# A fused decoder layer: the state sums on two column tiles of TensorE, the heads spread by pairs of chunks and sequence, and the second head's turning placed behind the first quadrants

## The chip, the core and the metric

The kernel runs on one core of a Trainium2 chip. The time is the device time of one execution in microseconds (us). The engines are TensorE (PE in the profile, its weight loads PEld), VectorE (DVE), ScalarE (ACT), GpSimd (POOL) and SyncE (SP), which issues most DMAs. The kernel before took 1444.93 us, the median of three runs (1443.88 to 1446.36).

## The reference, cut to what matters

A post-norm decoder layer over 16 sequences of 256 tokens with 512 features, in float32. Each of three sublayers is added to its input and layer-normalised.

```python
# 1: a state-space mixer inside
xn = x * rsqrt(mean(x*x)) * w_norm
z, xi, dt, B, C = split(xn @ W_in.T)           # z, xi: 1024 wide; dt: 16 heads; B, C: 16 heads x 16 states
xi = silu(causal_conv4(xi)); dt = softplus(dt + dt_bias); dA = exp(dt * -exp(A_log))
u = (dt * mean_over_64_channels(xi))[..., None] * B
h_t = dA_t * h_(t-1) + u_t                     # a scan along the tokens of a sequence
y_t = sum over the 16 states of h_t * C_t      # 16 heads per token
y = (y @ W_h2i.T) * silu(z)                    # 16 heads -> 1024 channels
out = y @ W_out.T + x
# 2: a long convolution along the 512 features, per position in a head of 8 tokens
# 3: x @ W.T + b + a top-2 mixture of 8 rank-16 updates
```

What the change touches most are the three lines of the sum over the states, the spreading of 16 heads to 1024 channels, and the gate by `silu(z)`.

## The kernel before, in words

**First stage** (span 0 to about 771 us). The 4096 tokens go in eight groups of 512, that is two sequences of 256 at a time. For each group ten pairs of products (`first_products`, `last_products`, line 309) make `xi`, `z`, `B` and `C`, with the channels (or the heads' states) on the 128 partitions and the 512 tokens along the free axis. They are Strassen-like products of 256 columns each. A product of two chunks of `z` is called a pair `p`; its chunks are `2p` and `2p+1`. The order of the ten pairs is a list in the code (lines 576, 577), and each step issues, by hand, the first products of its own pair, the last products of the pair before, and the vector work between. No scheduler reorders anything: each engine takes its instructions in the order in which the code issues them.

Three small steps sit between these products on TensorE:

- `head_means` (line 550) makes means over 64 channels, with weights of 32 columns, in four column tiles of the array side by side.
- The state sums, `yps` (line 611). After the scan, `Bs[ht]` holds the products of state and `C` for 8 heads x 16 states on 128 partitions (`ht` is 0 or 1). A 0/1 matrix `sel` adds up the 16 states of each head. It has four copies of the 32 columns, so the 128 output partitions hold the same sums four times. These are two matmuls of the full array, 512 columns each. ScalarE copies the result to `yT` (line 639).
- `spread_heads(cc)` (line 668), once for each half of the 1024 channels. Chunk `4cc+q` takes rows `32q` to `32q+31` of `yT` (copy `q`) against 32 rows of `w_h`, in four row tiles side by side, into four PSUM banks. `gated` (line 681) multiplies each chunk of `z` with one bank on VectorE.

Then comes the output projection (line 709), again in the Strassen-like form, and the layer norm. The eighth group has nothing to overlap with, so it uses the plain product (line 795) over four token tiles in the order 0, 2, 1, 3, then VectorE adds the residual and normalises (`L810`, `L61`, `L501`), and SP stores to DRAM. Within the fourth tile TensorE also turns (transposes) the first head's input, `turned_v`, line 146; ScalarE copies it (line 148), and VectorE makes its products with the context (line 158).

**Second stage** (from about 771 us). Over 32 heads: a convolution as a Toeplitz product, `convolve`, for each of two halves of the batch. It has twelve *quadrants* (64 x 64 tiles, line 977) and full-array matmuls (line 959). In the first half of the first head (`late`) the quadrants come first and six full matmuls (`FIRST`) behind them. VectorE then contracts the result with the context (lines 1010 and 1020). A head's input is loaded by `load_v` (one buffer, so the next load waits for the turning of the last), turned, and multiplied one head ahead. Before the first head's loop begins, the second head's input is turned (line 1108), and then the third head's input and context are loaded.

PSUM has eight banks: two of `ps_t` (tag `tr`), and in the first stage two of `ps_s` and four of `ps_mm` (`bank()`). In the second stage the two of `ps_b` and the four of `ps_y` (the tiles `y0` and `y1`) take the place of the last six.

The lines that the change and the steps of the prediction touch:

Of the kernel before, what the change touches and what calls it, by code (L numbers as in the profile page):

```python
# [14 lines left out]
P = 128  # L15
# [4 lines left out]
NI = DI // P  # L20
# [51 lines left out]
def decoder_kernel(  # L72
# [63 lines left out]
    def load_v(h):  # L136
        vn = q3.tile([P, D], F32, tag="vn", name="vn", bufs=1)
        sh, hs = divmod(h, P // NH)
        nc.sync.dma_start(vn, first[sh][:, hs * NH : (hs + 1) * NH, :])
        return vn  # L140
# [30 lines left out]
    with ExitStack() as s1:  # L171
# [3 lines left out]
        p2 = s1.enter_context(tc.tile_pool(name="p2", bufs=2))  # L175
        gp = s1.enter_context(tc.tile_pool(name="gp", bufs=NI))
        ps_s = s1.enter_context(tc.tile_pool(name="ps_s", bufs=2, space=PSUM))
# [70 lines left out]

        w_h = w1.tile([P, 2, P], F32, name="w_h")
        nc.gpsimd.memset(w_h, 0.0)  # L250
        for q in range(4):
            nc.sync.dma_start(
                w_h[32 * q : 32 * q + H1],
                Wh2iT.rearrange("h (cc q i) -> q h cc i", q=4, i=P)[q],
            )
# [44 lines left out]

        sel = w1.tile([P, HT, 4, 2 * H1], F32, name="sel")
        nc.gpsimd.memset(sel, 0.0)

        def bank():
            return ps_mm.tile([P, 512], F32, tag="mm", name="mm")
# [142 lines left out]
        for ht in range(HT):  # L448
            for q in range(4):
                nc.vector.tensor_reduce(  # L450
                    sel[:, ht, q, ht * HH : (ht + 1) * HH],
                    ident.rearrange("p (h n) -> p h n", n=NST),
                    AX.X,
                    ALU.add,
                )
# [51 lines left out]
        for g in range(NG):  # L507
# [5 lines left out]

            accs, zs, silus = [], [], []

            def places(kind, p):

                if kind == "x":
                    two = [t[:, :, 3:] for t in (xis[2 * p % 4], xis[2 * p % 4 + 1])]
                    return [t[:, b, :] for t in two for b in range(GB)]  # L520
                if kind == "z":
                    two = [gp.tile([P, GT], F32, tag="zs", name="zs") for _ in range(2)]
                    zs.extend(two)
                else:
                    two = [p2.tile([P, GT], F32, tag=kind, name=kind) for _ in range(2)]
                    (Bs if kind == "b" else Cs).extend(two)
                return [t[:, b * S : (b + 1) * S] for t in two for b in range(GB)]
# [69 lines left out]
            for i, (kind, p) in enumerate(order):  # L597
# [9 lines left out]
                if i == 9:  # L607

                    yps = ps_t.tile([P, GT], F32, tag="tr", name="yps")
                    for ht in range(HT):  # L610
                        nc.tensor.matmul(  # L611
                            yps,
                            sel[:, ht].rearrange("p q h -> p (q h)"),
                            Bs[ht],
                            start=(ht == 0),
                            stop=(ht == HT - 1),
                        )
                if before is not None:
# [18 lines left out]
                if i == 9:  # L637
                    yT = q3.tile([P, GT], F32, tag="vn", name="yT", bufs=1)
                    nc.scalar.copy(yT, yps)
# [24 lines left out]
            def spread_heads(cc):  # L664
                pss = []
                for q in range(4):
                    ps = bank() if q < 2 else ps_t.tile([P, GT], F32, tag="tr", name="wh")
                    nc.tensor.matmul(  # L668
                        ps,
                        w_h[32 * q : 32 * (q + 1), cc, :],  # L670
                        yT[32 * q : 32 * (q + 1), :],
                        start=True,
                        stop=True,
                    )
                    pss.append(ps)
                return pss

            def gated(cc, pss):
                for q in range(4):
                    z = zs[4 * cc + q]  # L680
                    nc.vector.tensor_tensor(z, z, pss[q], ALU.mult)

# [104 lines left out]
            else:  # L787
                finish_sums()
                gated(1, spread_heads(1))
                for n, t in enumerate((0, 2, 1, 3)):  # L790

                    ps = ps_s.tile([P, 512], F32, tag="s", name="s") if n == 0 else bank()
                    for c in range(NI):
# [43 lines left out]
    with ExitStack() as s2:  # L837
# [111 lines left out]

        def convolve(y, kv, T, Td, kvd, q, between=None, late=False, early=None):  # L950

# [48 lines left out]
            if late:  # L1000
                for n, (lb, mb) in enumerate(FIRST):
                    if n == 1 and early is not None:
                        early()
                    if n == 3 and between is not None:
                        between()
                    full(lb, mb, T[:, FULL_AT[lb, mb], :])
# [100 lines left out]
        more_next[3]()  # L1107
        vT_after = turned_v(vns.pop(0))
        vns.append(load_v(2))
        cTs.append(load_c(2))  # L1110

# [26 lines left out]
        for h in range(HX):  # L1138
# [33 lines left out]
            red = p2.tile([P, NQ, NL, BQ * NH], F32, tag="red", name="red")  # L1172
            convolve(y, kv, T, Td, kvd, 0, late=h == 0)
            ws = skip_sum(sk_next)
# [201 lines left out]
```

## Time and profile before

| | us |
|---|---|
| median of three runs | 1444.93 |
| the profiled execution's own time | 1447.89 |
| its span (first to last instruction) | 1446.1 |
| one group of the first stage, in the steady part | 92.45 |
| TensorE busy | 1425.9 (99%) |
| VectorE busy | 1215.7 (84%) |
| ScalarE busy | 464.4 (32%) |
| GpSimd busy | 567.8 (39%) |

The profiled execution is 1.8 us longer than its span, and 2.96 us above the median of the runs. Each float32 matmul of the program appears as two matmuls, two passes, in the profile: `yps` has 16 in the program and 32 in the profile. The mean duration of one matmul in a group includes the way out of the array and overlaps the next, so that what a matmul costs is read from the chain of waits, where pieces lie end to end: `PE mm L309 x16` in 3.45 us is 0.2156 us for a pass of 256 columns. The granted clock of TensorE is 0.998 of full speed.

### The profile page before, as it was taken

Reading aid. Unit: us, or ns where it says so; the run is one execution under the profiler, and the core shown is the slowest. Engines: PE = TensorE matmul, PEld = TensorE weight load, DVE = VectorE, ACT = ScalarE, POOL = GpSimd, SP = SyncE. Lnnn points to the kernel's source line nnn. Section 1 sums busy time; section 2 is a strip of 40 time slices with the busy share of each in tenths; the row PEclk is TensorE's granted clock in tenths of the full one; section 3 lists DMA queues with packets and bytes.
Section 4 is the critical chain, followed back from the end, with each engine's and each line's share of the span. In section 5 each row is a group of like instructions: output and inputs, shape, how many; then the busy total and the mean of one; then the engine's idle time right before and its main releaser. Section 6 shows DMA issues by size and latency. Waiting matters only on the chain.

```text
span 1446.1 us, 18895 instructions
## 1 busy us (share of the span) xinstructions
PE 1425.9 (99%) x6828; PEld 915.6 (63%) x6828; DVE 1215.7 (84%) x2093; ACT 464.4 (32%) x969; POOL 567.8 (39%) x662
## 2 busy tenths in 40 slices
PE   8999999999999999999999999999999999999997
PEld 8778788788887888878875444444444444444443
DVE  6877778878787787877857999999999999999996
ACT  2522223223233232332311333333333333333332
POOL 7340010020100201002004666776677666766772
PEclk9999999999999999999999999999999999999999
DMA  8014012111121111202103122212221222122210
GB/s 295 32 37 130 8 39 81 44 54 36 37 83 38 53 44 37 83 11 84 51 8 120 42 80 73 69 61 79 74 76 54 79 73 70 58 81 73 68 40 23
DMA packets 50815, 93.30 MB, mean 65 GB/s; under 512 B 10657, under 2 KB 15009, under 8 KB 50721
## 3 DMA queue, kind: packets, MB, share of 16 engines
q1 hardware_dynamic: 50192, 92.08, 19.9%
q8 instruction: 54, 0.88, 0.3%
q14 instruction: 41, 0.33, 0.1%
q10 hardware_dynamic: 528, 0.00, 0.0%
HBM read 74.75 MB, written 17.32 MB: 64 GB/s over the span
## 4 chain that ended last, share of the span: by engine, by line
PE 90%; DVE 6%; issue 1%; DMA 1%; ACT 1%; POOL 0%; SPq 0%; POOLq 0%; DVEq 0%; ACTq 0%
PE mm L309 18%; PE y L959 15%; PE s L309 12%; PE y L977 12%; PE base L1133 8%; PE s L709 6%; PE mm L709 5%; PE yc L947 4%; PE gl L1198 2%; PE base L1129 2%; DVE acc L540 2%; PE tr L1047 1%; PE mm L795 1%; PE mm L668 1%; PE yps L611 1%
## 5 line engine op out<-in xcount | busy, mean ns | idle before, releaser
L1010 DVE TENSOR_TENSOR pr<-y,cT 128x1024 f32<-128x1024 f32 x126 | 148.3, 1219 | 41.5 <-PE y L977 37.1
L977 PE MATMUL y<-kv 64*64 64x512 f32 x1408 | 180.8, 598 | 0.5 <-DVE xt L810 0.4
L158 DVE TENSOR_TENSOR kv<-vT,cT 128x1024 f32<-128x1024 f32 x128 | 180.0, 1447 | 1.4 <-ACT vT L148 1.4
L540 DVE SCALAR_TENSOR_TENSOR acc<-xi,wc,acc 128x512 f32<-128x512 f32 x192 | 145.9, 774 | 5.7
L1020 DVE TENSOR_REDUCE red<-pr 128x128 f32<-128x1024 f32 x126 | 147.1, 1208 | 0.0
L959 PE MATMUL y<-kv 128*128 128x512 f32 x272 | 128.1, 594 | 2.1 <-DVE pr L1010 1.2
L977 PEld LDWEIGHTS y<-kv 64*64 64x64 f32 x1408 | 51.5, 132 | 120.6 <-issue 91.0
L885 POOL TENSOR_TENSOR o<-t,vT 64x384 f32<-64x384 f32 x64 | 121.1, 1892 | 4.4
L1133 PE MATMUL base<-w_f,ol 128*128 128x512 f32 x248 | 119.5, 605 | 0.0
L959 PE MATMUL y<-kv,Td 128*128 128x512 f32 x248 | 116.5, 592 | 0.0
L357 POOL TENSOR_TENSOR rstd<-ms,nhalf 128x4 f32<-128x4 f32 x8 | 8.1, 1018 | 260.1 <-DVE ms L355 260.1
L67 POOL TENSOR_TENSOR rs_a<-ve_a,nhalf 128x1 f32<-128x1 f32 x32 | 19.0, 593 | 189.0 <-DVE ve_a L65 189.0
L309 PE MATMUL mm<-XT,w_z 128*128 128x256 f32 x384 | 90.7, 379 | 0.0
L959 PEld LDWEIGHTS y<-kv,Td 128*128 128x128 f32 x248 | 47.1, 190 | 59.3 <-issue 59.1
L959 PEld LDWEIGHTS y<-kv 128*128 128x128 f32 x272 | 49.0, 190 | 53.9 <-issue 50.6
L924 POOL TENSOR_TENSOR xs<-kv 128x512 f32<-128x512 f32 x63 | 80.4, 1276 | 2.4
L309 PEld LDWEIGHTS mm<-XT,w_z 128*128 128x128 f32 x384 | 73.0, 190 | 9.9
L1133 PEld LDWEIGHTS base<-w_f,ol 128*128 128x128 f32 x248 | 42.3, 189 | 54.5 <-issue 54.5
L948 ACT COPY y<-yc 128x1024 f32<-128x1024 f32 x62 | 61.8, 997 | 34.0 <-PE yc L947 23.8
L1165 POOL TENSOR_TENSOR ol<-o,red 128x512 f32<-128x512 f32 x31 | 39.5, 1273 | 83.3 <-DVE red L1020 83.3
L309 PE MATMUL mm<-xnT,w_z 128*128 128x256 f32 x288 | 70.4, 381 | 0.0
L977 PE MATMUL y<-kvd,kv 64*64 64x512 f32 x128 | 65.2, 589 | 0.0
(276 smaller groups left out, 2957.2 us busy)
## 6 DMA issues: line engine op xcount, KB each, us to landing
cT<-in_ctxT SPq DMA_DIRECT2D x32, 448.0 KB
kv<-in_toep SPq DMA_DIRECT2D x32, 448.0 KB
xt<-in_x SPq DMA_DIRECT2D x32, 256.0 KB
xnT<-in_xT SPq DMA_DIRECT2D x8, 1024.0 KB
spread<-both SPq DMA_DIRECT2D x32, 256.0 KB
first<-xt SPq DMA_DIRECT2D x32, 256.0 KB
vn<-first SPq DMA_DIRECT2D x32, 256.0 KB
out<-res SPq DMA_DIRECT2D x31, 256.0 KB
```

Source lines behind the costliest of these rows:

```text
L158: last = nc.vector.tensor_tensor(kv[:, q, k * BQ : (k + NL // 2) * BQ], vT[:, q, blks].rearrange("p k (b i) -> p (k b) i", i=NH).unsqueeze ...
L309: nc.tensor.matmul(ps, w[:, p, a, kc, :], Xs[b][:, kc, :], start=start and kc == 0, stop=stop and kc == 1, skip_group_check=upon,)
L540: nc.vector.scalar_tensor_tensor(acc, xi[:, :, k : k + S], wc[:, c, k : k + 1], acc, ALU.mult, ALU.add)
L709: nc.tensor.matmul(ps, own[a][c][:, n * P : (n + 1) * P], w_o[b][c], start=start and c == 0, stop=stop and c == HC - 1, skip_group_check=upon,
L885: nc.gpsimd.tensor_tensor(o[b : b + HP, :, 0:3], t[a : a + HP, :, 1:4], vT[a : a + HP, :, 1:4], ALU.add,)
L924: return nc.gpsimd.tensor_tensor(xs[:, q], moving(kv, q, 0), moving(kv, q, 1), ALU.add)
L948: nc.scalar.copy(y[1], yc.unsqueeze(1).to_broadcast([P, 2, BQ * NH * NH]))
L959: nc.tensor.matmul(bank_of(y, lb), w, moving(kv, q, mb), start=not late and lb not in begun, stop=False, skip_group_check=True,)
L977: return nc.tensor.matmul(bank_of(y, lb)[cols], T[rows, at, cols], src[rows], start=start, stop=False, skip_group_check=True,)
L1010: nc.vector.tensor_tensor(pr.rearrange("p (k b j) i -> p k b j i", k=2, j=NH), y[i].rearrange("p k (b j i) -> p k b j i", j=NH, i=NH), cT[ ...
L1020: nc.vector.tensor_reduce(red[:, q, 2 * i : 2 * i + 2, :].rearrange("p k t -> p (k t)"), pr, AX.X, ALU.add)
L1133: nc.tensor.matmul(base, o_l[:, kc, :], w_f[:, kc, :], start=(first and kc == kcs[0]), stop=False)
```

## The change

- **State sums.** `sel` keeps two copies of the 32 columns instead of four, so that a sum takes 64 columns of the array. Each of the two matmuls of 512 columns becomes two of 256: sequence 0 goes to column tile 0 (output partitions 0 to 63), sequence 1 to column tile 1 (64 to 127). `yps` and `yT` are 256 wide instead of 512.
- **Spreading.** A row tile `q` now stands for a sequence (`q // 2`) and a pair of chunks (`q % 2`). `w_h` holds two chunks for each row tile (loaded twice, once per sequence), and each row tile makes two matmuls of 256 columns in place of one of 512, into the two halves of its bank.
- **Gating.** The two chunks of a pair of `z` lie in one tile `[P, 2, 512]`, and `gated` multiplies, for one sequence, both chunks of a pair at once: 2 x 256 elements in place of 512 in a row.
- **The last group's fourth token tile** uses the free bank of `ps_s` in place of one of `ps_mm`.
- **The second head's turning**, with the two loads behind it, is issued behind the twelve quadrants of the first head's first half (a callback `ahead`), ahead of the six full matmuls, instead of before the quadrants.

```diff
-        gp = s1.enter_context(tc.tile_pool(name="gp", bufs=NI))
+        gp = s1.enter_context(tc.tile_pool(name="gp", bufs=NI // 2))
...
-        w_h = w1.tile([P, 2, P], F32, name="w_h")
+        w_h = w1.tile([P, 2, 2, P], F32, name="w_h")
         nc.gpsimd.memset(w_h, 0.0)
         for q in range(4):
             nc.sync.dma_start(
                 w_h[32 * q : 32 * q + H1],
-                Wh2iT.rearrange("h (cc q i) -> q h cc i", q=4, i=P)[q],
+                Wh2iT.rearrange("h (cc q e i) -> q h cc e i", q=2, e=2, i=P)[q % 2],
             )
...
-        sel = w1.tile([P, HT, 4, 2 * H1], F32, name="sel")
+        sel = w1.tile([P, HT, 2, 2 * H1], F32, name="sel")
...
-            for q in range(4):
+            for q in range(2):
                 nc.vector.tensor_reduce(sel[:, ht, q, ...], ...)
...
-                    two = [gp.tile([P, GT], F32, tag="zs", name="zs") for _ in range(2)]
+                    pair = gp.tile([P, 2, GT], F32, tag="zs", name="zs")
+                    zpairs.append(pair)
+                    two = [pair[:, e, :] for e in range(2)]
...
-                    yps = ps_t.tile([P, GT], F32, tag="tr", name="yps")
+                    yps = ps_t.tile([P, S], F32, tag="tr", name="yps")
                     for ht in range(HT):
-                        nc.tensor.matmul(
-                            yps,
-                            sel[:, ht].rearrange("p q h -> p (q h)"),
-                            Bs[ht],
-                            start=(ht == 0),
-                            stop=(ht == HT - 1),
-                        )
+                        for b in range(GB):
+                            nc.tensor.matmul(
+                                yps[b * HP : (b + 1) * HP],
+                                sel[:, ht].rearrange("p q h -> p (q h)"),
+                                Bs[ht][:, b * S : (b + 1) * S],
+                                start=(ht == 0),
+                                stop=(ht == HT - 1),
+                            )
...
-                    yT = q3.tile([P, GT], F32, tag="vn", name="yT", bufs=1)
+                    yT = q3.tile([P, S], F32, tag="vn", name="yT", bufs=1)
...
             def spread_heads(cc):
-                pss = []
-                for q in range(4):
-                    ps = bank() if q < 2 else ps_t.tile([P, GT], F32, tag="tr", name="wh")
-                    nc.tensor.matmul(
-                        ps,
-                        w_h[32 * q : 32 * (q + 1), cc, :],
-                        yT[32 * q : 32 * (q + 1), :],
-                        start=True,
-                        stop=True,
-                    )
-                    pss.append(ps)
+                pss = [
+                    bank() if q < 2 else ps_t.tile([P, GT], F32, tag="tr", name="wh")
+                    for q in range(4)
+                ]
+                for e in range(2):
+                    for q, ps in enumerate(pss):
+                        nc.tensor.matmul(
+                            ps[:, e * S : (e + 1) * S],
+                            w_h[32 * q : 32 * (q + 1), cc, e, :],
+                            yT[32 * q : 32 * (q + 1), :],
+                            start=(e == 0),
+                            stop=(e == 1),
+                            skip_group_check=True,
+                        )
                 return pss
 
             def gated(cc, pss):
-                for q in range(4):
-                    z = zs[4 * cc + q]
-                    nc.vector.tensor_tensor(z, z, pss[q], ALU.mult)
+                for q, ps in enumerate(pss):
+                    b, k = divmod(q, 2)
+                    z = zpairs[2 * cc + k][:, :, b * S : (b + 1) * S]
+                    nc.vector.tensor_tensor(z, z, ps.rearrange("p (e s) -> p e s", e=2), ALU.mult)
...
-                    ps = ps_s.tile([P, 512], F32, tag="s", name="s") if n == 0 else bank()
+                    ps = ps_s.tile([P, 512], F32, tag="s", name="s") if n in (0, 3) else bank()
...
-        def convolve(y, kv, T, Td, kvd, q, between=None, late=False, early=None):
+        def convolve(y, kv, T, Td, kvd, q, between=None, late=False, early=None, ahead=None):
...
                 for n, (lb, mb) in enumerate(FIRST):
+                    if n == 0 and ahead is not None:
+                        ahead()
...
-        vT_after = turned_v(vns.pop(0))
-        vns.append(load_v(2))
-        cTs.append(load_c(2))
+        vT_ahead = []
+
+        def ahead():
+            vT_ahead.append(turned_v(vns.pop(0)))
+            vns.append(load_v(2))
+            cTs.append(load_c(2))
...
-            convolve(y, kv, T, Td, kvd, 0, late=h == 0)
+            convolve(y, kv, T, Td, kvd, 0, late=h == 0, ahead=ahead)
+            if h == 0:
+                vT_after = vT_ahead[0]
```

More of the change, by code (lines that the diff above doesn't have):

```diff
@@ L512, in decoder_kernel @@
                 cTs = [load_c(0), load_c(1)]
-            accs, zs, silus = [], [], []
+            accs, zs, zpairs, silus = [], [], [], []
             def places(kind, p):
```

## The prediction, made before the changed kernel was run

> **What bounds the kernel now.** The page first, for the bound:
>
> ```profile
> PE 1425.9 (99%) x6828; PEld 915.6 (63%) x6828; DVE 1215.7 (84%) x2093; ACT 464.4 (32%) x969; POOL 567.8 (39%) x662
> ```
>
> TensorE is busy nearly always, so time taken from it counts wherever nothing else ends later. The chain of waits says where that is. In the seventh group it runs on TensorE alone (start, length, piece):
>
> ```profile
> 633.72 1.00 PE xm L550 x8
> 634.72 2.79 PE mm L309 x12
> 637.50 3.45 PE s L309 x16
> 640.96 1.72 PE yps L611 x4
> 642.67 2.59 PE mm L309 x12
> 645.26 0.63 PE mm L668 x2
> ...
> 645.90 0.41 PE mm L668 x2
> ...
> 646.33 2.79 PE s L309 x12
> ```
>
> Three things are to be read here. A pass of 256 columns on the full array costs 3.45 / 16 = 0.2156 us, one of 512 columns 1.72 / 4 = 0.43. Tiles side by side do overlap: `xm` makes eight passes of 512 in 1.00, not 3.44. And tiles cost a switch on both sides: `xm` takes 1.00 where two rounds of 0.43 would be 0.86 (0.14 for going in), and the twelve products behind it take 2.79 where twelve behind `yps` take 2.59 (0.20 for coming out). `spread_heads` pays the same: 1.07 for 0.86, then again 2.79.
>
> Next, all engines in a small window of the timeline, for the weight loads of one spread:
>
> ```profile
> 645.19 0.19 PEld L668 LDWEIGHTS mm<-yT,w_h 32*128 32x128 f32 x2 [0.33 <-issue]
> ...
> 645.31 0.19 PEld L668 LDWEIGHTS wh<-yT,w_h 32*128 32x128 f32 x2
> ```
>
> Between these two lines stand two for `wh` at 645.20 and two more for `mm` at 645.30. Eight loads of 0.19 start within 0.12 us.
>
> Last, the passage between the stages, where the turning is moved: the chain, then TensorE's timeline with its idle time in brackets.
>
> ```profile
> 769.25 3.48 DVE kv L158 x3
> ...
> 780.76 2.28 DVE pr L1010 x2
> ...
> 783.14 1.00 ACT y L948
> ```
>
> ```profile
> 771.32 0.66 PE L146 MATMUL tr<-ident,vn 128*128 128x128 f32 x4 [0.41 <-DMA vn<-first]
> ...
> 773.39 1.50 PE L977 MATMUL y<-kv 64*64 64x512 f32 x10 [0.42 <-DVE xt L810]
> ...
> 784.19 1.13 PE L959 MATMUL y<-kv 128*128 128x512 f32 x2 [0.94 <-ACT y L948]
> ```
>
> This chain begins with the first head's turning at 767.02 and its copy on ScalarE, ready at 768.08. From there to 783 the end is set by VectorE, not by TensorE: the four products of the first head, the last residual and norm, two products of the second head, then the contraction, all in VectorE's own order. TensorE idles 0.41 for the load of the second head and 0.42 for a PSUM bank, and all the same arrives early enough to wait 0.94 at 784.19.
>
> **The change, part by part.**
>
> *State sums.* Removed: four passes of 512, 1.72 us. Added: eight of 256 columns in two column tiles, four rounds, 4 x 0.2156 = 0.86, plus the two sides of the switch, 0.14 + 0.20 (rows `xm` and the 2.79). That is 1.20, or 0.52 less per group. Everything behind `yps` in a group follows from TensorE (the next products, the spread, the gates), and ahead of it VectorE has `Bs` ready at 639.65, 1.3 us early, so the whole 0.52 counts in a steady group. In the first group `yps` waits 1.79 for VectorE, but what it then takes is on the chain just the same (76.87, 1.96 us). Eight groups: 8 x 0.52 = **4.2 us less**. From both sides: were the switch free it would be 8 x 0.86 = 6.9 less; were the two tiles not to overlap, 1.72 + 0.34, 8 x 0.34 = 2.7 more. I take the middle value, as `xm`, the 32-column sums of `d_lg` (32 passes of 128 columns in 1.01, eight rounds of 0.108) and `spread_heads` all overlap and all pay 0.14 to 0.2 going in.
>
> The rule that speaks against this step is in the Trainium skill, "TensorEngine Tiling (Array Packing)", section Tiling Modes: changing the mode, not merely the tile, drains TensorE. It gives no price; the rows above show the drain, and by the page's own "up to 2x" for 64 columns with no drain the sum would be 6.9 less instead of 4.2.
>
> *Copy to `yT`.* 512 to 256 columns on ScalarE, 0.59 to about 0.37 (the copy of 128 x 256 at line 331). It runs at 642.71 and is needed at 645.26, so it is worth nothing; without its 2 us of cover it would give 0.2 per group.
>
> *Spreading.* Four matmuls of 512 become eight of 256, so the passes per row tile go from 2 x 0.43 to 4 x 0.2156, the same 0.86. The loads double from 8 to 16 per spread, in 16 spreads. On the full array a 128-column load hides wholly under a 256-column pass (0.2156 per pair of load and pass), and the second four loads above start 0.11 after the first four, under the first passes. I take 0. Upper end: each of the two added rounds shows one load of 0.11, 0.21 per spread, 3.4 us in all. Lower end: 0, since neither columns nor a switch are saved.
>
> On loads the Trainium skill ("TensorE: Matmul & The Clock Gate", section "LDWEIGHTS (loading the stationary operand)") says that a load's time goes by its columns, so that a 32 x 128 load costs as much as a full one; the rows agree (0.182 against 0.190). Worked out from that page, 128 / 1.2 = 107 ns each, sixteen loads in a line would be 1.71 us, an estimate, and the sum 9.4 us more instead of 4.2 less. "TensorEngine Tiling (Array Packing)" of the same skill (Key Properties) has tiles loading in parallel, as the four starts at one time do.
>
> *Gating.* The same four operations per half, 512 elements each, as 2 x 256 with a stride. The four-tap operations on 2 x 256 (line 540) take 0.774 where a plain one of that kind (line 386) takes 0.744, so at most 0.03 each, 0.12 for four. What is queued behind: the second spread needs the first gates' banks. They end at 648.83 and it starts at 649.05, a cover of 0.2; cost nothing, or 0.1 x 8 if it is gone. The second of the later gates now needs chunks 6 and 7 at 651.4, and ScalarE's last Silu ends at 651.50: 0.1 of VectorE's time, with TensorE covered until 657.29 by 32 products while the sums it needs end at 654.56.
>
> *Set-up.* `sel` takes four reductions of 0.2 less on VectorE, which then idles 3.53 until 7.63; the memset of `w_h` grows by some 0.2 ahead of the identity, whose first use (the warming matmuls, from 1.59) ends well before 8.96. The four small loads of `w_h` stay four on SP, and are needed at 81. Nothing. Some 14 first matmuls now also wait for an older matmul on the same PSUM slot, long done; a separate wait takes 0.05 on PE's queue (line 611 has such ones, without a gap in the chain), at most 0.7.
>
> *The turning, and the bank.* After: TensorE ends the products at 770.9 and starts the quadrants at once (the first two products of VectorE end at 770.4, and the banks of `ps_mm` are free). They take 2.74, to 773.65, then the turning 0.6, to 774.25, its load long landed (771.3). The twelve full passes of 0.43 end at 779.4, not 781.3. So TensorE gains 1.9 and gives it back: `y0` may be overwritten only once VectorE has read it at 781.9, and the seeding copy comes at 784.14 as before, behind 768.11 to 783.04 of VectorE's work, of which nothing is shortened. Late next: nothing; the second head's copy moves from 772.87 to about 774.9 and VectorE asks for it at 777.41. SP has the two loads behind the store of line 503 (776.92) and issues them at 777.8 in both. ScalarE's small copy that releases the last quadrants comes behind its second `kvd` copy (772.26), in time for 772.8. I take 0; bounds: 1.9 less if VectorE's chain gives way, 0.5 more if the turning's switch shows at 784.
>
> The idle time of TensorE there becomes 1.9 and 1.1 us in two pieces. In the first group 1.79 idle ahead of `yps` are followed by twelve products in 2.59, full speed, so I price this at nothing. (The Trainium skill, "TensorE: Matmul & The Clock Gate", section "Why this matters for your kernels", sets the limit at about 3 us of idle time; no gap here is that long.)
>
> *Sum.* -4.2 + 0 + 0 + 0. The profiled execution was 1447.89, 2.96 above the median: it becomes 1443.7, and the median 1444.93 - 4.2 = **1440.8 us** (-0.29%). A measurement of this kernel tells 0.2%, 2.9 us, from no change.
>
> **The rivals.**
>
> 1. *The switch is free* for two column tiles: 6.9 less, 1438.0. For it: going in and out overlap with other waits in the first group. Against: columns of 32, rows of 32 and the quadrants' 64 x 64 (2.74 us for 24 passes of 512, 2.58 without a switch) all pay it in this profile.
> 2. *The added loads show* in the spreads, 0.21 each: 3.4 given back, 0.8 less, 1444.1. For it: no row here has 128-column loads in row tiles under passes as short as 0.2156. Against: the starts 0.11 apart.
> 3. *The passage gains too*: VectorE's chain is not the bound there, 1.9 more gained, 1438.9. Against: the chain above.
> 4. *The columns don't overlap*, so that the step doesn't do what it is for: 2.7 more, 1447.6. Against: `xm` and the quadrants (24 passes of 512 in 2.74).
> 5. *The loads go one after the other* (slower): sixteen at 0.11 make a spread 1.76 + 0.2, 0.9 more, 16 x 0.9 = 14.4, together 10.2 more, 1455.1. It decides from (4.2 + 2.9) / 16 = 0.44 more per spread, that is 1.5 us. Against: four tiles' loads start within 0.01.
>
> **How the numbers follow.** Forecast 0.55 (1439.3 to 1442.3 by itself), rival 1 0.10, rival 2 0.15, rival 3 0.08, rival 4 0.05, rival 5 0.07. Faster by over 0.2%: 0.50 of the forecast, 1 and 3 whole, 0.68. Within 0.2%: 0.05 of the forecast, 2 whole, 0.03 of 4, 0.23. Slower: 5, and 0.02 of 4, 0.09. The range runs from rival 1 less 1 us for the runs' own spread (1437.0) to rival 2 plus 1.4 (1445.5) and leaves out 4 and 5.
>
> **What would show it.** In the changed profile `yps` takes 1.0 in the chain and the products behind it 2.79; a steady group takes 91.93 in place of 92.45; the spreads stay at 1.07; TensorE's two waits of 0.4 near 771 are gone, and the second stage still waits on the seeding copy some 13 us behind the first products. Wrong if a spread takes 1.2 or more, if `yps` stays at 1.7, or if the group moves by another amount than `yps` does.

## The result, and the profile after

The changed kernel takes **1440.79 us** (median of 12 runs, 1440.41 to 1443.65) against 1444.76 us of the kernel before (12 runs beside it, 1443.88 to 1446.36). The ratio is 0.9976, with an interval of 0.9967 to 0.9985: 0.24% faster. The forecast was 1440.8. The median fits, but as will be seen not every step behind it does, and the 12 runs are of two kinds: seven lie at 1440.4 to 1441.0 and five at 1442.0 to 1443.7. The profiled execution is the slowest of the 12, 1443.65 (span 1441.8).

The page of the changed kernel, share of the span and instructions of each engine:

```profile
PE 1421.7 (99%) x6988; PEld 918.0 (64%) x6988; DVE 1216.1 (84%) x2089; ACT 462.6 (32%) x969; POOL 567.3 (39%) x662
```

TensorE has 160 instructions more (32 for the sums, 128 for the spreads) and 4.2 us less of busy time. The chain of waits of the changed kernel in the seventh group (start, length, piece) is where the change was to be read:

```profile
631.07 3.45 PE s L310 x16
634.52 1.01 PE yps L616 x8
635.54 2.79 PE mm L310 x12
638.33 0.41 PE mm L677 x2
...
638.97 0.20 PE mm L677 x2
...
639.40 2.79 PE s L310 x12
```

`yps` takes 1.01 where it took 1.72, the twelve products behind it 2.79 where they took 2.59, and the spread 1.07 (638.33 to 639.40) as before. The piece `yps` of the group before starts at 542.57 in the same view, so a steady group takes 91.95; it took 92.45.

The first group is different. The timelines of TensorE there, of the kernel before and of the changed one, idle time in brackets with what ended it:

```profile
88.72 1.97 PE L709 MATMUL s<-w_o_sum,z_sum 128*128 128x256 f32 x8 [0.46 <-DVE zs L346]
```

```profile
88.61 1.75 PE L719 MATMUL s<-w_o_sum,z_sum 128*128 128x256 f32 x7 [0.94 <-DVE zs L347]
```

TensorE saves its 0.5 here too and then waits 0.5 longer, since `z_sum` and the gated chunks of VectorE end when they did. `yps` starts at 76.87 and 76.86, so the first group gives 0.1, not 0.5.

Now the passage between the stages. TensorE's timeline of the changed kernel:

```profile
766.16 0.66 PE L146 MATMUL tr<-ident,vn 128*128 128x128 f32 x4
766.65 5.32 PE L970 MATMUL y<-kv 128*128 128x512 f32 x12
771.80 1.02 PE L958 MATMUL yc<-xs,kv 128*128 128x512 f32 x2
774.54 1.13 PE L970 MATMUL y<-kv 128*128 128x512 f32 x2 [1.72 <-DVE pr L1023]
776.77 2.07 PE L970 MATMUL y<-kv 128*128 128x512 f32 x2 [1.11 <-ACT y L959]
778.64 3.62 PE L970 MATMUL y<-kv,Td 128*128 128x512 f32 x4
```

The two waits of 0.4 are gone, and all that was gained is waited away at 774.54 and 776.77 (1.72 and 1.11). What was not expected are the last two lines: two passes take 2.07 and four take 3.62, twice their time. The busy times of that place by stretch (behind the length comes TensorE's busy time, and the number ahead of the last two is its granted clock) name the cause:

```profile
772.69:776.10 3.41, 1.26 (x3) 0.30 (x2) 3.41 (x4) 0.38 (x1) 2.51 (x3) 1.00 0.45 154
776.10:779.51 3.41, 2.74 (x4) 1.19 (x5) 3.41 (x4) 0.62 (x1) 3.27 (x3) 0.50 0.00 0
779.51:782.93 3.42, 3.42 (x8) 0.96 (x10) 1.73 (x2) 0.00 (x0) 2.26 (x3) 0.50 0.00 0
782.93:786.34 3.41, 3.41 (x28) 1.13 (x21) 0.85 (x1) 1.33 (x3) 1.09 (x1) 1.00 0.00 0
```

From 776.10 to 782.93 the granted clock is half. (Why the stretches are cut at just these times is told under "The wait filled".) In the chain of waits the stretch from the seeding copy to the products behind the next contraction becomes 11.2 us (776.77 to 788.00); it was 8.2 (784.19 to 792.42). So this execution loses 3.0 us here.

One more place differs, and it is the other way round. VectorE's timelines in the second group, before and after:

```profile
132.18 0.63 DVE L483 TENSOR_TENSOR w_f<-w_f,ident 128x64 f32<-128x64 f32 x4 [1.97 <-DMA w_f<-in_WffnT]
```

```profile
129.92 0.63 DVE L484 TENSOR_TENSOR w_f<-w_f,ident 128x64 f32<-128x64 f32 x4
```

The profiled execution of the kernel before waits for the load of the weight `w_f`. TensorE's timeline there shows what follows, and the stretches show why it is more than the wait:

```profile
133.60 2.57 PE L309 MATMUL mm<-xnT,w_xi 128*128 128x256 f32 x8 [1.99 <-DVE u L332]
```

```profile
131.70:135.12 3.42, 1.52 (x7) 1.17 (x7) 2.80 (x11) 0.23 (x1) 0.00 (x0) 1.00 0.65 199
135.12:138.53 3.41, 3.41 (x10) 2.69 (x9) 1.95 (x6) 1.28 (x4) 0.00 (x0) 0.50 0.36 133
```

TensorE stands still for 1.99 and then runs at half clock for 3.41. In the timeline, from `yps` of the first group to `yps` of the second this execution takes 101.65 us, the changed kernel's 97.80: 3.7 us, beside the 0.1 above, that have nothing to do with the change.

So the two profiled executions differ by 4.24 us for these reasons: seven groups at 0.5 and one at 0.1, 3.6 less; no late `w_f`, 3.7 less; half clock in the passage, 3.0 more. That is 4.3. The forecast's 4.2 between the two executions is met by chance, and the experiments have to say which part belongs to the change.

### The profile page after: what moved, and what is told of

Its sections match the earlier page's. It is cut to its first block, busy times and chain, and to the rows that moved or that the text cites. A ratio compares the mean times of both kernels' runs of the same rounds, so it can differ in the third digit from the quotient of the medians.

```text
span 1441.8 us, 19197 instructions
## 1 busy us (share of the span) xinstructions
PE 1421.7 (99%) x6988; PEld 918.0 (64%) x6988; DVE 1216.1 (84%) x2089; ACT 462.6 (32%) x969; POOL 567.3 (39%) x662
## 4 chain that ended last, share of the span: by engine, by line
PE 91%; DVE 5%; issue 1%; DMA 1%; POOL 1%; ACT 1%; SPq 0%; POOLq 0%; DVEq 0%; ACTq 0%
PE mm L310 18%; PE y L970 15%; PE s L310 12%; PE y L988 12%; PE base L1149 8%; PE s L719 6%; PE mm L719 6%; PE yc L958 4%; PE gl L1216 2%; PE base L1145 2%; DVE acc L543 2%; PE tr L1060 1%; PE mm L677 1%; PE xm L553 1%; PE mm L806 1%
## 5 line engine op out<-in xcount | busy, mean ns | idle before, releaser
L1033 DVE TENSOR_REDUCE red<-pr 128x128 f32<-128x1024 f32 x126 | 147.1, 1209 | 0.0
```

The source lines that it names most:

```text
L1033: nc.vector.tensor_reduce(red[:, q, 2 * i : 2 * i + 2, :].rearrange("p k t -> p (k t)"), pr, AX.X, ALU.add)
```

## The experiments

Two theories stand at the start. *Theory A*: the column tiles give all of the gain, and the turning with its bank gives nothing but the risk of the half clock. *Theory B*: the turning gains in itself and is only hidden by the clock. Beside them stand two questions: does the late `w_f` depend on the change, and does the size of the step carry further?

### The first stage alone

The changed kernel with the turning and the bank as they were:

```diff
-ps = ps_s.tile(...) if n in (0, 3) else bank()
+ps = ps_s.tile(...) if n == 0 else bank()
-def ahead():
-    vT_ahead.append(turned_v(vns.pop(0)))
-    ...
+vT_after = turned_v(vns.pop(0))
+...
```

> The changed kernel with the second head's turning and the last bank put back as before: the state sums, the spreads and the gates alone. The theory after the result: the column tiles give the whole 4.2 us (yps 1.01 in place of 1.72, 0.20 for coming out), and the moved turning only adds a stretch at half clock in those runs (5 of 12) that lie at 1442 to 1443.7. It expects 1440.5 in every run, a clock of 0.998 in every run, and no pass of 0.9 us near 777. Rival: the half clock belongs to the column tiles or to chance, and then some runs here lie at 1442 or above too. Second rival: the turning and the bank gave part of the 4.2, then this lies at 1441.5 or more in all runs.

Measured: 1440.51 (six runs, 1440.07 to 1440.86), ratio 0.9967 (0.9955 to 0.9979) against 1445.43 beside it. TensorE's timeline in the passage, one wait and full speed:

```profile
776.65 1.12 PE L970 MATMUL y<-kv 128*128 128x512 f32 x2 [0.93 <-ACT y L959]
777.61 1.88 PE L970 MATMUL y<-kv,Td 128*128 128x512 f32 x4
```

It is as fast as the faster runs of the whole change, and none of its six runs lies higher. The whole gain is that of the first stage, and there the steady group moves by what the sums on column tiles take less.

### The turning alone

The kernel before with `ahead` and the bank of the change, and its first stage untouched:

```diff
-ps = ps_s.tile(...) if n == 0 else bank()
+ps = ps_s.tile(...) if n in (0, 3) else bank()
-convolve(y, kv, T, Td, kvd, 0, late=h == 0)
+convolve(y, kv, T, Td, kvd, 0, late=h == 0, ahead=ahead)
```

> The kernel before with only the turning moved behind the quadrants and the fourth token tile in the free bank. The prediction's step (TensorE gains 1.9 and gives it back) expects 1444.8, no difference, and TensorE waiting about 1.7 and 1.1 us at the start of the second stage. The half-clock theory expects the same in most runs and 1.5 to 3 us more in some, with a clock of 0.996 or 0.997 in those. The rival that the passage gains expects 1442.9.

Measured: 1445.63 (eleven runs, seven at 1444.18 to 1445.66, four at 1446.98 to 1448.76), ratio 1.0005 (0.9996 to 1.0013). Its timeline has the same two waits, in this execution with the clock at full speed:

```profile
778.70 1.13 PE L959 MATMUL y<-kv 128*128 128x512 f32 x2 [1.71 <-DVE pr L1012]
780.94 1.13 PE L959 MATMUL y<-kv 128*128 128x512 f32 x2 [1.11 <-ACT y L948]
```

No gain, so theory B falls. The four high runs fit a clock that falls in some executions, but the late `w_f` can make such runs as well, so this kernel does not settle that.

### The wait filled

The changed kernel, with eight products of the identity with itself, whose result nothing uses, in the place of the wait of 1.72:

```diff
+if h == 0:
+    keep = ps_b.tile([P, D], F32, tag="base", name="keep")
+    for _ in range(8):
+        nc.tensor.matmul(keep[:, 0:P], ident, ident, start=True, stop=True)
```

> The changed kernel with eight added matmuls of 128 x 128 on the identity into an idle bank (their result is used by nothing), behind the seeding product of the first head, where TensorE waits 1.72 us for VectorE: 16 passes of 0.108, 1.7 us. The half-clock theory expects every run at 1440.5 with 0.998, no slow runs any more, because the idle time is filled and VectorE sets the end there. If idle time has nothing to do with it, some 4 runs in 10 stay at 1442 or above. If the filler delays the chain, all runs rise by up to 0.5.

Measured: 1440.93 (six runs, 1440.44 to 1441.56), ratio 0.9969 (0.9958 to 0.9981). Of the two waits only that of 1.11 is left, the passage keeps the full clock, and no run reaches 1442. TensorE does more and the high runs are gone.

To have this side by side on one chip, the changed kernel, the filler and a third form (turning where it was, only the bank of the change kept) ran once more together:

```diff
-ps = ps_s.tile(...) if n == 0 else bank()
+ps = ps_s.tile(...) if n in (0, 3) else bank()
```

> The changed kernel once more, on the same chip as the three runs beside it. The half-clock theory expects two clusters as in the first comparison: some 6 in 10 runs at 1440.5 with a clock of 0.998 or 0.999, the others at 1442 to 1443.7 with 0.996 or 0.997. If the slower cluster was chance of that one chip, all lie at 1440.5.

> The changed kernel with the second head's turning before the quadrants again, but the fourth token tile kept in the free bank. The 0.42 us for the bank is gone, so TensorE ends its first full passes some 0.4 earlier and waits that much longer for VectorE: about 1.4 and 1.1 us, against 0.9 in one piece in the first stage alone and 1.72 and 1.11 in the changed kernel. Median 1440.5, as nothing here sets the end. If it is the sum of both waits that drops the clock, the slower cluster appears here in fewer runs than in the changed kernel, if at all; if the turning itself does it, never.

> The changed kernel with the 1.72 us wait filled by eight idle matmuls, on the same chip as the changed kernel. Half-clock theory: no run of the slower cluster (none in six so far), median 1440.5 to 1440.9. Rival: the share of slow runs is that of the changed kernel beside it.

Measured: the changed kernel 1442.38 (eleven runs, three at 1440.43 to 1441.09, eight at 1442.16 to 1443.93); the bank alone 1440.89 (seven runs, six at 1440.17 to 1441.13, one at 1442.27); the filler 1440.78 (seven runs, 1440.53 to 1441.04). The profiled executions, first the changed kernel's, TensorE's timeline and two stretches:

```profile
774.34 1.12 PE L970 MATMUL y<-kv 128*128 128x512 f32 x2 [1.70 <-DVE pr L1023]
776.57 1.13 PE L970 MATMUL y<-kv 128*128 128x512 f32 x2 [1.11 <-ACT y L959]
```

```profile
770.66:774.07 3.41, 1.97 (x5) 0.57 (x3) 3.41 (x3) 0.00 (x0) 2.25 (x2) 1.00 0.95 275
774.07:777.49 3.42, 2.04 (x4) 0.79 (x5) 3.42 (x4) 1.00 (x1) 3.13 (x5) 1.00 0.08 31
```

the bank alone, the same two views:

```profile
774.65 1.13 PE L970 MATMUL y<-kv 128*128 128x512 f32 x2 [1.31 <-DVE pr L1023]
776.89 2.07 PE L970 MATMUL y<-kv 128*128 128x512 f32 x2 [1.11 <-ACT y L959]
```

```profile
773.11:776.52 3.41, 1.35 (x3) 0.30 (x2) 3.41 (x4) 0.68 (x1) 2.77 (x4) 1.00 0.34 123
776.52:779.94 3.42, 3.05 (x4) 1.50 (x5) 3.42 (x4) 0.31 (x1) 3.34 (x3) 0.50 0.00 0
```

and the filler:

```profile
777.00:780.00 3.00, 3.00 (x10) 1.17 (x14) 3.00 (x3) 0.00 (x0) 2.92 (x3) 1.00 0.00 0
```

The changed kernel here has the very waits of its first profile and keeps the clock, so the same waits bring the half clock in one execution and not in the next. With the waits at 1.31 and 1.11 it came in the profiled execution, at 1442.27, for 3.41 us instead of 6.83. Counting runs at 1442 and over: 13 of 23 with waits of 1.7 and 1.1, one of 7 with 1.3 and 1.1, none of 13 with 1.1 alone, none of 6 with 0.93 alone (the first stage alone). Two of the high runs were traced, and both show the half clock; that it is the cause in the other 12 is inferred from their times and mean clocks (0.996 or 0.997).

What differs from execution to execution can be read from the traces, though no run was made to test it. All changes of the granted clock in one trace lie whole multiples of 3.413 us apart (in the first trace of the changed kernel at 4.69, 776.10, 782.92 and 1438.28, that is 226, 2 and 192 steps), and this grid begins at another place of the kernel in each trace. The stretches above are cut at it. In the changed kernel's first trace one stretch holds the whole wait of 1.72 and part of the next: TensorE is idle for 2.15 of 3.41, and the half clock follows. In its second trace the grid cuts the first wait, and two stretches have 1.44 and 1.38 idle. With the bank alone it is 2.06 in one stretch, and the clock falls. Over all 14 traces, between 10 and 1424 us, a stretch at full clock with 1.89 idle or more was followed by the half clock in four cases of four, one with 1.80 in one of five, and one with less in none. At the kernel's end 1.59 to 1.72 was enough in three traces. After a fall the clock came back behind one stretch, and in the changed kernel's first trace, where that one has 0.67 idle, behind two. Were each place of the grid as likely, an estimate from 1.89 and these waits would give the half clock to some 4 runs in 10 with 1.7 and 1.1, to 3 in 10 with 1.3 and 1.1, and to none with 1.1 alone; counted were 13 of 23, 1 of 7 and 0 of 13.

### The late load of `w_f`

The kernel before once more, to have its trace without the late load.

> The kernel before, once more, for a second profile. In the first one VectorE waited 1.97 us for the load of w_f at 132 and TensorE stood still behind it, and that execution was 3 us above the median. The theory that this wait is chance of that one execution expects none here, a time of 1444 to 1445 on execution without profile and the first products of group 2 some 3.4 us earlier than in the first profile. If the wait belongs to the kernel it is here again.

Measured: 1444.26. There is no wait for `w_f`, and from the first to the second `yps` it takes 97.9. Against this execution the first stage alone (1440.51) is 3.75 us faster, close to the 3.6 of the groups.

Why the load comes late in one program rather than the other is seen in SP's own timeline, in the same group, of the kernel before and then of the first stage alone:

```profile
112.54 1.73 SPq L430 DMA_DIRECT2D both<-two  x4
117.38 1.83 SPq L442 DMA_DIRECT2D spread<-both  x3
```

```profile
112.07 1.73 SPq L431 DMA_DIRECT2D both<-two  x4
114.97 1.84 SPq L443 DMA_DIRECT2D spread<-both  x3
```

SP is 1.9 us later in the kernel before, and the loads of `w_gl` and `w_f` stand behind that in its queue. All traces of programs with the old first stage show 4.1 to 4.8 us between these two starts, all with the new one 2.9; what holds SP was not tried. The lateness alone does not make the wait: the second trace of the kernel before has 4.2 and no wait. It issues the load of `w_f` at 120.72 where the first issues it at 122.65, and the programs with the new first stage at 118.8 to 120.2; in the first trace the load took 9.51 from there to its landing. To take the wait away in both, `w_f` was asked for later:

```diff
-if g == 1 and i == 2:
+if g == 1 and i == 4:
     with_identity(w_f)
```

> The kernel before with one edit: in group 2 VectorE adds the identity to w_f two steps later (before the fifth pair of products, not the third), so that it comes some 12 us later than the load that it waits for. The theory that part of the measured difference is this wait (2 us in the first profile of before, 0.6 in the one with the turning only, none in the three of the changed kernels) expects 1444.3 in every run and no run above 1444.8, the median 0.3 to 1.1 under that of the kernel before. The rival that the spread of the kernel before (1443.9 to 1447.8) has other causes expects no change.

> The state sums, spreads and gates of the change, the turning as before, and w_f used two steps later as in the run beside it. Against that run it shows the column tiles alone, without the wait: 7 groups x 0.50 and 0.1 in the first make 3.6 us, so 1440.6 against 1444.3. If the wait never bit in the changed kernel, it equals the run with the first stage only, 1440.5, within 0.3.

Measured: the kernel before with it 1444.35 (eleven runs, 1443.98 to 1445.28, two of them above the expected limit of 1444.8; ratio 0.9997, 0.9988 to 1.0006), the first stage alone with it 1441.24 (ten runs, 1440.76 to 1441.83). So the column tiles are worth 3.1 here, not the 3.6 expected, and the edit is not neutral: it makes a new wait where `w_f` is first used. TensorE's timelines of the two:

```profile
141.47 3.67 PE L491 MATMUL mw<-w_f,share 128*128 128x512 f32 x8 [0.96 <-issue]
```

```profile
140.28 3.67 PE L492 MATMUL mw<-w_f,share 128*128 128x512 f32 x8 [0.39 <-DVE w_f L484]
```

It takes the late load from the one, and costs the other a wait that it had not had: 0.39 in this trace, 0.7 between the medians of the two sets of runs. How many runs of the kernel before have the late load stays open: the 0.5 between the medians with and without the edit (1444.89 and 1444.35) is less than a measurement can tell.

### The order of issue

Is the overlap of the column tiles a matter of alternating them? The two tiles of the first stage alone, one after the other in the code:

```diff
-for ht in range(HT):
-    for b in range(GB):
+for b in range(GB):
+    for ht in range(HT):
```

> The first stage of the change, but the sums are issued tile by tile: both matmuls of sequence 0, then both of sequence 1. If each tile takes its own work from a queue that looks ahead, yps stays at 1.01 in the chain. If the array takes the passes strictly in order and overlaps only neighbours on different tiles, the four passes of one tile end before those of the other begin, yps takes 1.0 + 0.65 or more, and a group grows by 0.65.

Measured: 1440.57 in one run, and in the chain of waits:

```profile
542.50 1.02 PE yps L616 x8
543.52 2.79 PE mm L310 x12
```

In a steady group the order makes no difference: four rounds of 0.2156 and the way in are all that `yps` takes, so the second tile's work overtakes the first's. In the first group it does make one, in the same view:

```profile
76.67 1.59 PE yps L616 x8
```

With alternating tiles this piece takes 1.16. There the second matmul of each tile waits for VectorE's `Bs[1]`, and the eight passes start one, one, two, two, one, one, as if the first tile's waiting matmul held up the second tile's, whose data lay ready. It costs nothing in the end, since VectorE ends that group: from these sums to the next it takes 97.90, and 97.83 with alternating tiles.

### Four column tiles

If two tiles give 0.5 per group, four should give more: `yps` in tiles of 32 output rows, 128 tokens each, and the spread in four passes of 128 columns.

```diff
-for b in range(GB):
-    nc.tensor.matmul(yps[b * HP : (b + 1) * HP], ..., Bs[ht][:, b * S : (b + 1) * S], ...)
+for b in range(4):
+    nc.tensor.matmul(yps[32 * b : 32 * (b + 1)], sel[:, ht], Bs[ht][:, b * P : (b + 1) * P], ...)
-for e in range(2):
+for e in range(4):
     for q, ps in enumerate(pss):
-        nc.tensor.matmul(ps[:, e * S : (e + 1) * S], ...)
+        nc.tensor.matmul(ps[:, e * P : (e + 1) * P], ...)
```

It was made from the first stage alone, with `w_f` at the later place, and with the load of `b_bc` moved to the start of the second stage to make room; then once more with `w_f` at its old place.

> The same step carried on: the sums on four column tiles of 32, one per quarter of 128 tokens, and a spread in which a row tile is a quarter of the tokens and makes four matmuls of 128 columns (one per chunk of its half). The turning is as before, w_f is used two steps later, and the bias of the feed-forward is loaded at the start of the second stage to make room. Sums: 16 passes of 128 columns, four rounds of 0.108, 0.43 + 0.14 going in in place of 1.01, 0.44 less per group. The spread has eight rounds of 0.108 and 32 loads of 128 columns: if loads of a tile hide under passes of their own length it stays at 1.07, and the time is 1437.2 (8 x 0.43 under 1440.6). If a pair of load and pass costs 0.19, a spread takes 1.7 and the time is 1440.6 - 3.4 + 16 x 0.65 = 1447.

> The four column tiles of 32 with w_f used where the kernel before uses it. Using it two steps later had cost 0.4 to 1.0 us at the product with w_f that follows (TensorE waits there in all three profiles), so this should take back about 0.5: 1436.8. If the load of w_f comes late here, as in some runs of the kernel before, it is 1437.3 or more.

Measured: **1437.33** (five runs, 1437.14 to 1437.62; ratio 0.9950, 0.9936 to 0.9964) and 1437.38 (five runs, 1436.34 to 1437.81; 0.9946, 0.9933 to 0.9958). Both beat the kernel before and the changed one. The chain of waits of the first:

```profile
541.70 0.57 PE yps L615 x16
542.27 2.79 PE mm L310 x12
545.06 0.31 PE mm L676 x2
...
546.16 2.79 PE s L310 x12
```

`yps` goes from 1.01 to 0.57, and a spread takes 1.10 instead of 1.07, though its loads have doubled again to 32. A steady group takes 91.57 or 91.58: 0.38 less, as 0.44 less twice 0.03. But the sum does not come from there alone. From the first group to the second this kernel takes 98.46 where the first stage alone takes 97.82, so that at the end of its wait of 0.93 in the passage it is 1.91 us ahead (774.74 against 776.65), and it ends 3.3 ahead in the trace. (The first stage alone with `w_f` at the later place, as here, takes 98.19 from the first group to the second, and ends the same wait 2.2 behind the quarters.) The rest arises in the second stage, in one instruction. The same line of VectorE (count, then shortest, median and longest in ns) in the kernel before (traced again), the first stage alone, and the quarters:

```profile
L1069 DVE SCALAR_TENSOR_TENSOR ex<-rank,ex x32: 168/197/1273, 805.7 to 1433.5; 128x8 f32<-128x8 f32 x32
```

```profile
L1082 DVE SCALAR_TENSOR_TENSOR ex<-rank,ex x32: 168/198/1279, 801.8 to 1429.8; 128x8 f32<-128x8 f32 x32
```

```profile
L1078 DVE SCALAR_TENSOR_TENSOR ex<-rank,ex x32: 166/197/202, 799.8 to 1426.4; 128x8 f32<-128x8 f32 x32
```

One of 32 takes 1.27 us instead of 0.20. It is on the chain: the block that holds it takes 21.9 us where the others take 20.6. In the traces of programs with the old first stage it is the block that starts near 1209, in those with the column tiles of 64 the one near 855, in both traces of the quarters there is none. So 1.3 of the quarters' gain is a stall that this program happens not to have, and the tiles' own part is 1.9 to 2.2. That the time comes out at the expected 1437.2 is thus chance: 3.4 was expected of the tiles. That the earlier `w_f` gives the supposed 0.5 was not shown. Its profiled execution loses the clock in the first group; three of its five runs have a mean clock of 0.997 and lie at 1437.38 to 1437.81, the two others at 1436.34 and 1436.71.

## Why the prediction was right, and where it was not

- **State sums, 4.2.** The mechanism is shown. A steady group gains 0.50 (0.52 forecast), `yps` takes 1.01 (1.00) and the products behind it 2.79 (2.79): the price of going in and of coming out, read off `xm`, holds for this shape too. The mis-sized term is the first group, counted at 0.52 and worth 0.1. "What it then takes is on the chain just the same" was true up to the products that wait for `z_sum`, where VectorE's 0.46 of lateness became 0.94. The sum is 3.6. That the median still came out as forecast has luck in it: between medians the first stage is worth anything from 3.1 (both with the later `w_f`) to 4.9 (the first stage alone), and what the kernel before loses beyond the 3.6 in its median run was not shown.
- **Spreading, 0.** Shown twice, with 16 loads (1.07) and with 32 (1.10). The Trainium skill says in "TensorEngine Tiling (Array Packing)", section Key Properties, that tiles load in parallel; the runs agree, and the reading of the start times was the better guide than the sum of load lengths. Rivals 2 and 5 fall, as rivals 1 and 4 do with `yps` at 1.01.
- **Copy, gating, set-up, 0.** The steady group moves by what the sums alone explain, 0.50, so nothing of these shows there, and the first `yps` starts at 76.86 where it started at 76.87, so nothing of the set-up either.
- **Turning and bank, 0.** Right for the chain: VectorE sets the end, TensorE's gain turned into waits of 1.72 and 1.11 (1.9 and 1.1 forecast), and the turning alone gains nothing. Rival 3 falls.
- **"So I price this at nothing."** This clause of the turning failed. In 13 of 23 runs the time is 1.5 to 3.4 us above the 1440.5 of the others, and the median of the second set of runs (1442.38) is 1.6 above the forecast; the first set's median happened to fall among the undisturbed ones. The row that I leant on was one execution. With the same gap of 1.8 us ahead of the first group's `yps`, the traced filler kernel shows this in its chain and stretches:

```profile
77.31 1.16 PE yps L616 x8
78.47 4.47 PE mm L310 x12
```

```profile
75.33:78.75 3.42, 1.62 (x11) 0.75 (x11) 3.28 (x10) 0.23 (x1) 0.83 (x1) 1.00 0.00 0
78.75:82.16 3.41, 3.41 (x10) 2.69 (x9) 0.40 (x1) 0.52 (x2) 3.41 (x6) 0.50 0.07 1
```

  Twelve products in 4.47, not 2.79. Two of the 14 traces have this dip (this one and the quarters with `w_f` early, where the stretch ahead has 1.80 and 1.89 idle), all 14 have the gap. What failed is the rule behind the clause, one gap at a time with its length: the idle time of neighbouring gaps adds up within a stretch of the grid, 1.72 and part of 1.11 to 2.15. The limit of about 3 us that the Trainium skill gives ("TensorE: Matmul & The Clock Gate", section "Why this matters for your kernels") does not hold as a safe bound here: after 1.8 us the clock falls sometimes, and the measurement decides.
- **The base of the sum.** The profiled execution of before stood 2.96 above its median, and I carried that difference over unread. It was the late `w_f` and the half clock behind it, 3.7 us, which the timelines of TensorE and VectorE near 132 us show. The forecast of 1443.7 for the profiled execution after the change was met (1443.65) by chance: it has no late load, and the half clock in the passage took its place.

## What to carry to other kernels

Price a new idle gap of TensorE together with its neighbours: here the idle time within one stretch of 3.41 us went with the fall of the clock, from about 1.8 us. Where the stretches begin changes from run to run, so look at several executions: one trace that kept its speed proves little. Work taken from the busiest engine is worth its time only where no other engine ends at the same moment, so go through the groups one by one, the first above all. Where narrow outputs leave columns of the array unused, more and narrower tiles paid, and the price was 0.34 to 0.35 per round trip with two tiles as with four.

## What the runs showed of the hardware that I had not expected

- **The clock falls after short gaps, by their sum on a grid.** A half clock of 3.41 or 6.83 us followed gaps of 1.7 and 1.1 us with 1.1 of work between them in one of three traces, 1.3 and 1.1 in one of one, a gap of 1.8 alone (ahead of the first `yps`) in two of 14, and one of 2.0 alone (the late `w_f`) in one of one. Six traces have a gap of 1.5 to 2.0 that ends near 9 us, at the kernel's start, with no fall behind it; the grid of 3.413 us leaves at most 1.58 of it in one stretch. Gaps of 0.9 or 1.1 alone in the passage were followed by full speed in all ten traces that have them. Idle time of 1.89 or more in one stretch of the grid, and once of five times 1.80, is what the falls between 10 and 1424 us have in common. This is read from 14 traces, and no run was made to test it.
- **One slow instruction whose place goes with the program.** The `ex` of VectorE above, 1.27 us instead of 0.20 in one block of the second stage, at the same block in all traces of kernels with the same first stage, and SP's 1.2 to 1.9 us in the second group of the old ones, behave alike: they come at a fixed place in each program. That of the `ex` moved when only the first stage was changed, and in the quarters the stall is gone. A small change can so gain or lose 1.3 us at a place that it does not touch; what causes it stays open.
- **Loads of 128 columns all but hide under passes of 128 columns** when they go to four row tiles: a spread takes 1.10 with 32 loads, and 1.07 with 16.
